# A two-block transformer kernel: order of the first transfers and products, and buffers in two rings

## The chip, the cores and the metric

The kernel runs on one core of a Trainium2 chip. The metric is the device time of one execution in microseconds. Everything is fp32. A core has TensorE for matrix products (in the profile PE, with PEld for the loading of the stationary operand), VectorE (DVE), ScalarE (ACT), GpSimd (POOL), and the queue SyncE (SP), from which this kernel issues all its transfers.

## What is computed

Thirty-two sequences of 64 tokens, width 512, pass through two conditioned blocks. The first is an attention of 8 heads of width 64 that share one head of keys and values, with rotary positions read from an input, and then a gated MLP of width 2048. The second is an attention of 16 heads of width 32 with 4 groups of keys and values that come out of a latent of width 128. Both blocks add their result to their input. The reference, cut to this:

```python
# first block (RMS norm, scaled per sequence by the condition t)
h = rms(x) * (w1 * (1 + t @ tw1.T))
q, k, v = h @ Wq.T, h @ Wk.T, h @ Wv.T      # 8 heads of q, one of k and v
q, k = apply_rope(q, pos_ids), apply_rope(k, pos_ids)
x = x + softmax(q @ k.T / 8) @ v @ Wo.T
h = rms(x) * (w2 * (1 + t @ tw2.T))
x = x + (silu(h @ Wg.T) * (h @ Wu.T)) @ Wd.T
# second block (layer norm, scale and shift from t @ W_ada.T + b_ada)
h = layernorm(x) * (1 + scale) + shift
c = h @ Wkd.T                                # latent of 128
q, k, v = h @ Wq.T, c @ Wku.T, c @ Wvu.T     # 16 heads of q, 4 of k and v
x = x + softmax(rope(q) @ rope(k).T / sqrt(32)) @ v @ Wo.T
```

## The kernel before

**Units.** The 2048 tokens are cut into eight units of 256 tokens (four sequences); activations lie transposed, 128 features by 4 chunks by 256 tokens. `attention0(u)` is the first block's attention of unit u, `mlp(u)` its MLP, `attention1(u)` the second block. Each is a Python generator that records some instructions and yields at places where other work may be put in between. `Order.run` takes pieces of several generators in turn, by planned costs and latencies. The framework beneath then sets the order on each engine itself, following dependencies, its own estimates and the order in which the instructions were recorded; so the order of the trace isn't quite that of the program.

**MLP and its ring of sets.** The MLP uses a scheme of seven block products instead of eight. A set is 128 x 7 x 256 numbers of weight: three parts and four parts worked out from them and a fourth part `a21` (`combine`, L216 to L224, on POOL for the first two sets and otherwise three operations on DVE and one on POOL). In unit 0 a set is loaded as 384 KB (L208) and 128 KB (`a21`, L211, two buffers), combined, and its four worked-out parts are written to DRAM (L229, 512 KB). In the later units they are read back (L213) beside the 384 KB. A unit needs 24 sets, three for each of eight steps q: gate, up, and down of the step before. Sets sit in a ring of `MW = 4` buffers with the tag `mw` (L184); `done_with` asks for the set that goes into a freed buffer. The condition's weights `mod` 0 and 1 sit in the same four buffers before the sets.

**The head.** It runs from the start to the first product of the MLP. SP's transfers come in this order: `small` (condition, vectors, frequencies), `mod` 0, x of unit 0, positions (`pos`, L256), `wqkv` (the weights of queries, keys and values of the first block, 1280 KB in one transfer, L257), x of unit 1, `mod` 1, `wo0`, first sets, `mod` 2 and 3, then the weights of the second block and x of units 2 to 4. `modulation(i)` (L263) makes the scale vectors from the condition. `first_angles` (L339) makes the rotary angles of units 0 and 1 from the positions: about a dozen small operations each on DVE and ACT; `early` (L953) calls it within `attention0(0)`. `angles` (L293) does so for later pairs of units.

In the head both `attention0(0)` and `attention0(1)` are "lean". They square x on ACT (L474), scale x into `h` on DVE and POOL (L482), sum the squares on TensorE (`root_by_quarters`, L447), take the root on ACT (L444) and its reciprocal on DVE (L445), and spread cosine, sine and root over the partitions with small products (`tables_by_quarters`, L387, tiles `tab` and `row`). Only then are the products of queries recorded: first half, keys and values, second half (`project`, L499). Rotations (L507 to L510), transposed values `vt`, scores `sc` (L633), softmax (L519 to L529), transposed probabilities `pp` (L534), context `cx` (L650) and output `po` (L499) follow, then the second norm, whose root (`qs_b`, `row_b`) scales the operands of the MLP, `h` and `hc` (L495, L671 to L674).

The head's order comes from `order.run`: unit 0 has rank 1, unit 1 rank 2, the modulations 1 to 3 rank 3, until unit 0 is done. What is left of unit 1 runs beside `mlp(0)`. From then on `mlp(u)` runs with `attention0(u + 1)` and, one unit behind, `attention1(u - 1)`.

**The ring of x.** A unit's x stays in one of `XB = 5` buffers from its load to its second output store (L550) at the end of `attention1(u)`. `second` then asks for x of unit u + 5.

## Time and profile before

Three runs: median 1082.67 us (1082.35 to 1086.75). The profiled execution took 1086.17 us, of which 1084.1 are its span from the first instruction to the last; the rest lies around the span.

| | busy us | share of the span |
|---|---|---|
| PE (matrix products) | 1026.2 | 95% |
| PEld (weight loads, beside PE) | 948.3 | 87% |
| DVE | 548.7 | 51% |
| ACT | 322.5 | 30% |
| POOL | 434.1 | 40% |
| DMA, mean rate | 183 GB/s | |

The mean granted clock of TensorE is 0.989 of full speed. An engine's busy time is the union of its instructions' spans; matrix products are pipelined and their ends modelled, so a busy PE needn't be at its peak. The chain of waits follows the work back from the last instruction: 69% of it is PE, 11% DVE, 6% DMA, 5% POOL. A wait is put down to what ended last before it.

### The profile page before, as it was taken

The numbers are of one execution on the slowest core, as the hardware profiler recorded it, in microseconds if no ns is written. First come the engines' busy times: TensorE is split into PE (matmuls) and PEld (weight loads), VectorE is DVE, ScalarE is ACT, GpSimd is POOL, SyncE is SP. The second block draws the span as 40 slices with busy tenths as digits, with TensorE's granted clock in tenths as the row PEclk, the third lists the DMA queues.
The fourth block names the chain that finished last, engine by engine and source line by source line (L and its number), as shares of the span: only waits on it lengthen the run. The fifth ranks groups of instructions, "written<-read, shape, count | busy, mean of one in ns | idle before, by whom it ended". The sixth has DMA issues, their size and how long they took to land.

```text
span 1084.1 us, 21449 instructions
## 1 busy us (share of the span) xinstructions
PE 1026.2 (95%) x8538; PEld 948.3 (87%) x8538; DVE 548.7 (51%) x1377; ACT 322.5 (30%) x681; POOL 434.1 (40%) x520
## 2 busy tenths in 40 slices
PE   7899899999999989999999998999999999999887
PEld 6688899998999989999889897999899999998765
DVE  4866466543555475343654368432655344352363
ACT  4421122344124242133422323331424322141132
POOL 4424445443255434254343444324633244331441
PEclk8999999999999999999999999999999999999899
DMA  9717786353655454653646445455635556565001
GB/s 329 262 47 254 265 275 217 140 205 135 210 204 205 159 193 172 234 204 115 223 159 227 174 165 204 156 190 185 234 118 198 175 196 239 188 229 190 11 1 39
DMA packets 68130, 198.53 MB, mean 183 GB/s; under 512 B 7232, under 2 KB 15168, under 8 KB 67520
## 3 DMA queue, kind: packets, MB, share of 16 engines
q1 hardware_dynamic: 68032, 197.17, 52.1%
q8 instruction: 68, 1.11, 0.4%
q14 instruction: 30, 0.25, 0.1%
HBM read 180.37 MB, written 16.78 MB: 182 GB/s over the span
## 4 chain that ended last, share of the span: by engine, by line
PE 69%; DVE 11%; DMA 6%; POOL 5%; issue 2%; ACT 2%; SPq 0%; ACTq 0%; DVEq 0%; POOLq 0%
PE gu L838 27%; PE down L897 14%; PE po L499 10%; PE q L499 8%; DMA set<-in_wmlp 4%; DMA set<-sums 3%; PE pp L534 1%; PE lat L499 1%; PE cx L808 1%; PE sc L784 1%; PE cx L650 1%; DVE mx L519 1%; PE sc L633 1%; DVE sm L527 1%; DVE c L864 1%
## 5 line engine op out<-in xcount | busy, mean ns | idle before, releaser
L838 PE MATMUL gu<-h,set 128*128 128x128 f32 x2048 | 291.3, 278 | 11.8 <-DVE c L857 4.6
L838 PEld LDWEIGHTS gu<-h,set 128*128 128x128 f32 x2048 | 261.4, 193 | 19.3 <-issue 11.9
L838 PE MATMUL gu<-hc,set 128*128 128x128 f32 x1536 | 217.4, 277 | 4.6 <-DVE set L222 2.4
L838 PEld LDWEIGHTS gu<-hc,set 128*128 128x128 f32 x1536 | 194.5, 193 | 6.9 <-DVE set L222 3.6
L876 POOL TENSOR_TENSOR act<-c,c 128x384 f32<-128x384 f32 x64 | 66.5, 1040 | 206.8 <-DVE c L864 148.0
L897 PE MATMUL down<-td,set 128*128 128x128 f32 x1024 | 137.2, 276 | 6.3 <-DMA set<-sums 1.8
L897 PEld LDWEIGHTS down<-td,set 128*128 128x128 f32 x1024 | 125.0, 192 | 9.4 <-issue 3.7
L850 ACT COPY e<-gu 128x128 f32<-128x128 f32 x128 | 33.6, 264 | 303.6 <-PE gu L838 303.1
L499 PE MATMUL po<-cT,wo 128*128 128x256 f32 x480 | 110.8, 384 | 5.8 <-ACT cT L659 3.7
L864 DVE TENSOR_TENSOR c<-gu,u 128x256 f32<-128x256 f32 x128 | 53.4, 419 | 124.0 <-PE gu L838 123.9
L897 PE MATMUL down<-act,set 128*128 128x128 f32 x768 | 110.3, 279 | 3.5 <-DMA set<-in_wmlp 3.2
L852 DVE TENSOR_TENSOR u<-e,gu 128x128 f32<-128x128 f32 x128 | 36.0, 282 | 142.1 <-ACT e L850 141.5
L897 PEld LDWEIGHTS down<-act,set 128*128 128x128 f32 x768 | 97.8, 192 | 9.9 <-DMA set<-in_wmlp 5.8
L499 PEld LDWEIGHTS po<-cT,wo 128*128 128x128 f32 x480 | 90.2, 193 | 18.4 <-ACT cT L659 4.5
L529 POOL TENSOR_TENSOR p<-p,sm 128x512 f32<-128x512 f32 x40 | 40.9, 1042 | 120.2 <-DVE sm L528 114.3
L510 POOL TENSOR_TENSOR qT<-u_q,v_q 128x512 f32<-128x512 f32 x30 | 38.0, 1268 | 95.2 <-DVE v_q L509 95.2
L547 DVE TENSOR_TENSOR x<-x,po 128x512 f32<-128x512 f32 x32 | 22.0, 686 | 76.3 <-PE po L499 76.3
L499 PE MATMUL q<-h,wqkv 128*128 128x256 f32 x256 | 59.1, 382 | 0.8 <-ACT r_a L444 0.8
L933 ACT ACT_TABLE_LOAD x34 | 43.6, 1283 | 44.6 <-DVE c L864 44.3
L499 PEld LDWEIGHTS q<-h,wqkv 128*128 128x128 f32 x256 | 47.2, 190 | 7.4 <-ACT r_a L444 0.9
L499 PE MATMUL q<-h,wq 128*128 128x256 f32 x224 | 52.2, 385 | 1.6 <-POOL h L713 1.6
L878 POOL TENSOR_TENSOR td<-act 128x256 f32<-128x256 f32 x64 | 47.9, 749 | 9.9 <-DVE act L875 3.6
(275 smaller groups left out, 1404.3 us busy)
## 6 DMA issues: line engine op xcount, KB each, us to landing
set<-sums SPq DMA_DIRECT2D x168, 512.0 KB, 5.7
set<-in_wmlp SPq DMA_DIRECT2D x192, 384.0 KB, 4.6
sums<-set SPq DMA_DIRECT2D x24, 512.0 KB, 3.1
x<-in_x SPq DMA_DIRECT2D x8, 512.0 KB, 8.1
out_x<-x SPq DMA_DIRECT2D x16, 256.0 KB, 2.1
mod<-in_mod SPq DMA_DIRECT2D x7, 512.0 KB, 9.9
a<-in_wmlp SPq DMA_DIRECT2D x24, 128.0 KB, 2.9
wo<-in_wo SPq DMA_DIRECT2D x2, 1024.0 KB, 11.0
```

Of the source, the lines that this page charges most:

```text
L499: nc.tensor.matmul(ps, w[:, k, cols], h[:, k, :], start=(k == 0), stop=(k == KC - 1))
L510: nc.gpsimd.tensor_tensor(dst, u, v, ALU.add)
L529: nc.gpsimd.tensor_tensor(p8, p8, sm.unsqueeze(2).to_broadcast(wide), ALU.mult)
L547: nc.vector.tensor_tensor(x[:, part], x[:, part], po, ALU.add)
L838: nc.tensor.matmul(ps, w[:, slot, k * P : (k + 1) * P], b[of][:, k], start=start and k == 0, stop=k == 1, skip_group_check=True)
L850: nc.scalar.copy(e, ps[:, 0])
L852: nc.vector.tensor_tensor(u2, e, ps[:, 1], ALU.add)
L864: nc.vector.tensor_tensor(c.rearrange("p (a b) t -> p a b t", b=2)[:, :, 1], ps[:, 2:4], u2.unsqueeze(1).to_broadcast([P, 2, HT]), ALU.add,)
L876: nc.gpsimd.tensor_tensor(act[:, 1:4], gate[:, 1:4], c[:, 1:4], ALU.mult)
L878: nc.gpsimd.tensor_tensor(td[:, 0:2], act[:, 1:3], act[:, 0:2], ALU.subtract)
L897: nc.tensor.matmul(sums_of[u][p][:, c], w[:, slot, c * P : (c + 1) * P], b[of], start=q % NP == 0 and i % 2 == 0 and c == 0, stop=q % NP = ...
L933: nc.scalar.activation(gate[2][:, 0], gate[0][:, 0], AF.Silu)
```

## The change

- The positions are the first transfer of all. `first_angles` of units 0 and 1 is recorded ahead of `modulation(0)`, and the next pair's positions are asked for behind it.
- `wqkv` becomes two tensors: half of the queries with the keys and values (768 KB), and the other half of the queries (512 KB).
- In the lean units, keys and values and the first half of the queries are projected ahead of the tables; `query` returns its rotation as a function. The first norm's root gets its own small tile `few`. The two halves of the probabilities have a buffer each. The second norm's root and its spreading become two pieces with a yield in between.
- The head isn't planned by `order.run` any more. A string `FIRST` names, piece by piece, which of unit 0 (a), unit 1 (b) and the modulations 1 to 3 (m) is recorded next, and `ordered` ties TensorE's instructions of this stretch to the order of recording, by dependencies without a semaphore.
- The ring of sets has five buffers instead of four, that of x four instead of five.

```diff
+FIRST = "aaaaaaa bb a mm aa b a b aa bbb a b aa a bb a mmmm a bbbb".replace(" ", "")
...
+@contextmanager
+def ordered(tc, engine):
+    traced = tc.nc.cur_bb.bb.instructions
+    start = len(traced)
+    yield
+    mine = [i for i in traced[start:] if i.engine == engine]
+    info = mybir.DependencyInfo(mybir.DependencyClass.NoSync, mybir.DependencyReason.DATA)
+    for one, other in zip(mine, mine[1:]):
+        tc.add_manual_dep(other, one.name, info, reason="order")
...
+    load_positions(0)
     small = fixed("small", [P, C_ALL])
     nc.sync.dma_start(small, a["small"])
...
-    wqkv = fixed("wqkv", [P, KC, 640])
+    wqkv = [fixed("wqkv0", [P, KC, 384]), fixed("wqkv1", [P, KC, 256])]
...
-    XB = 5
+    XB = 4
...
-    MW = 4
+    MW = 5
...
     load_mod(0)
     load_x(0)
...
-    load_positions(0)
-    nc.sync.dma_start(wqkv, a["wqkv"])
+    for i, w in enumerate(wqkv):
+        nc.sync.dma_start(w, a[f"wqkv{i}"])
     load_x(1)
     load_mod(1)
...
+        if tag == "few":
+            return work({"0": "tot0", "1": "kr1"}[room["ring"]], [P, columns], name, 1)
...
         r = yield from norm
-
+        kv, turn = None, None
         if lean:
-            cos, sin, r = tables_by_quarters(u, r, room)
+            few = space(room, "few", 3 * S, f"quarters_{u}").rearrange("p (k c) -> p k c", c=S)
+            root_by_quarters(r, eps0, few[:, 0], f"ms_a{u}")
+            kv = keys_values()
+            yield 1.7, 0.0
+            turn = query(0)
+            yield 3.4, 0.0
+
+        if lean:
+            cos, sin, r = tables_by_quarters(u, few, room)
...
-        query(0)
-        yield 3.4, 0.0
-
-        kv = abank(f"kv0_{u}")
-        project(kv[:, :UT], wqkv, slice(D, D + P), h)
+        turn = turn or query(0)
+        turn(cos, sin)
+        yield 0.0 if lean else 3.4, 0.0
+
+        kv = kv or keys_values()
...
-        by_row(h, root_row(r, eps0, room, f"b{u}") if lean else r)
+        if lean:
+            root = space(room, "r", UT, f"r_b{u}")[:, :S]
+            root_by_quarters(r, eps0, root, f"qs_b{u}")
+            yield 0.3, 2.0
+            r = abank(f"row_b{u}")[:, :UT]
+            spread_out(r.rearrange("p (b s) -> p b s", s=S), root)
+        by_row(h, r)
...
     def early():
-        first_angles(0)
-        first_angles(1)
-        positions.pop()
-        load_positions(2)
         for z in (*vblk0, *vblk1):
             nc.gpsimd.memset(z, 0.0)
...
+    for u in range(2):
+        first_angles(u)
+    positions.pop()
     for _ in modulation(0):
         pass
+    load_positions(2)
...
-    head = [
-        Job(attention0(0, {"ring": "0", "lean": True}, early), A0, 1),
...
-    rest = order.run([*head, others], until=(head[0],))
...
+    ahead = Job(attention0(1, {"ring": "1", "lean": True}, late=lambda: angles(2)), A0)
+    streams = {
+        "a": attention0(0, {"ring": "0", "lean": True, "p": [first[:, :512], first[:, 512:]]}, early),
+        "b": ahead.pieces,
+        "m": other_mods(),
+    }
+    with ordered(tc, mybir.EngineType.PE):
+        for name in FIRST:
+            next(streams[name], None)
+    rest = [ahead]
```

More of the change, by code (lines that the diff above doesn't have):

```diff
@@ L1 @@
-from contextlib import ExitStack
+from contextlib import ExitStack, contextmanager
 import numpy as np
@@ L145, in two_blocks, with load_positions @@
     nc.gpsimd.memset(quarter, float(np.float32(np.pi / 2)))
+    positions = []
+    def load_positions(u0):
+        t = work("pos", [P, 2 * S], f"pos_{u0}", 1).bitcast(I32)
+        nc.sync.dma_start(t, a["pos"][:, u0 * S : (u0 + 2) * S])
+        positions.append(t)
+    load_positions(0)
     small = fixed("small", [P, C_ALL])
@@ L248, in two_blocks @@
     load_x(0)
-    positions = []
-    def load_positions(u0):
-        t = work("pos", [P, 2 * S], f"pos_{u0}", 1).bitcast(I32)
-        nc.sync.dma_start(t, a["pos"][:, u0 * S : (u0 + 2) * S])
-        positions.append(t)
-    load_positions(0)
-    nc.sync.dma_start(wqkv, a["wqkv"])
+    for i, w in enumerate(wqkv):
+        nc.sync.dma_start(w, a[f"wqkv{i}"])
     load_x(1)
@@ L385, in tables, with tables_by_quarters @@
         return cos, sin
-    def tables_by_quarters(u, parts, room):
-        few = work("pT0", [P, 512], f"quarters_{u}", 1).rearrange("p (k c) -> p k c", c=S)
+    def tables_by_quarters(u, few, room):
         r = few[:, 0]
-        root_by_quarters(parts, eps0, r, f"ms_a{u}")
         nc.vector.tensor_tensor(
@@ L557, in attention0, with query, turn, keys_values @@
         h = tile4(room, "h", f"h0_{u}")
+        def query(i):
+            q = abank(f"q0_{u}_{i}").rearrange("p (c t) -> p c t", c=2)
+            for c in range(2):
+                project(q[:, c], wqkv[i], slice(c * P, (c + 1) * P), h)
+            two = [P, 2, UT]
+            def turn(cos, sin):
+                cos, sin = (t.unsqueeze(1).to_broadcast(two) for t in (cos, sin))
+                rotate(qT[:, 2 * i : 2 * i + 2], q, cos, sin, two, f"q0_{u}_{i}")
+            return turn
+        def keys_values():
+            kv = abank(f"kv0_{u}")
+            project(kv[:, :UT], wqkv[0], slice(2 * P, 3 * P), h)
+            return kv
         norm = rms(u, s0a, h, room, f"a{u}")
@@ L570, in attention0 @@
         qT = tile4(room, "qT", f"qT0_{u}")
-        def query(i):
-            q = abank(f"q0_{u}_{i}").rearrange("p (c t) -> p c t", c=2)
-            for c in range(2):
-                project(q[:, c], wqkv, slice((2 * i + c) * P, (2 * i + c + 1) * P), h)
-            two = [P, 2, UT]
-            rotate(
-                qT[:, 2 * i : 2 * i + 2],
-                q,
-                cos.unsqueeze(1).to_broadcast(two),
-                sin.unsqueeze(1).to_broadcast(two),
-                two,
-                f"q0_{u}_{i}",
-            )
-        query(0)
-        yield 3.4, 0.0
-        kv = abank(f"kv0_{u}")
-        project(kv[:, :UT], wqkv, slice(D, D + P), h)
+        turn = turn or query(0)
+        turn(cos, sin)
+        yield 0.0 if lean else 3.4, 0.0
+        kv = kv or keys_values()
         ku = work("u", [P, 512], f"ku_{u}")[:HD0, :UT]
@@ L608, in attention0 @@
         nc.scalar.copy(kb[HD0:], kb[:HD0])
-        yield 1.7, 0.0
-        query(1)
+        yield 0.0 if lean else 1.7, 0.0
+        query(1)(cos, sin)
         yield 3.4, 0.0
@@ L620, in attention0 @@
         yield 0.3, 4.5
-        p = space(room, "p", 1024, f"p0_{u}").rearrange("p (c r k) -> p c r k", r=2, k=S)
+        if lean:
+            ps = [space(room, "p", 512, f"p0_{u}_{t}") for t in range(2)]
+        else:
+            both = space(room, "p", 1024, f"p0_{u}")
+            ps = [both[:, t * 512 : (t + 1) * 512] for t in range(2)]
         for ts in ((0,), (1,)) if lean else ((0, 1),):
@@ L639, in attention0 @@
                         )
-            softmax(banks, HD0**-0.5, f"0_{u}_{ts[0]}", p[:, KC * ts[0] : KC * (ts[-1] + 1)])
+            p = ps[ts[0]] if lean else both
+            softmax(banks, HD0**-0.5, f"0_{u}_{ts[0]}", p.rearrange("p (c r k) -> p c r k", r=2, k=S))
             yield 0.5 * len(ts), 5.0 * ts[0] if lean else 10.0
-        p = p.rearrange("p (t c) r k -> p t (c r k)", t=2)
         cT = tile4(room, "h", f"cT0_{u}")
         for t in range(2):
-            pT = turned(p[:, t], f"0_{u}_{t}", space(room, "pT", 512, f"pT0_{u}_{t}")).rearrange("p (c t) -> p c t", c=KC)
+            pT = turned(ps[t], f"0_{u}_{t}", space(room, "pT", 512, f"pT0_{u}_{t}")).rearrange("p (c t) -> p c t", c=KC)
             yield 0.5, 1.2
@@ L665, in attention0 @@
         r = yield from rms(u, s0b, h, room, f"b{u}")
-        by_row(h, root_row(r, eps0, room, f"b{u}") if lean else r)
+        if lean:
+            root = space(room, "r", UT, f"r_b{u}")[:, :S]
[4 more added lines that the diff above has]
+        by_row(h, r)
         sums = work("hc", [P, 3, 2, HT], f"hc_{u}", 2)
@@ L975, in two_blocks @@
     load_mod(3)
-    head = [
-        Job(attention0(0, {"ring": "0", "lean": True}, early), A0, 1),
-        Job(attention0(1, {"ring": "1", "lean": True, "p": [work("pw", [P, 1024], "p0_1", 1)]}, late=lambda: angles(2)), A0, 2),
-    ]
-    others = Job(other_mods(), 5.4, 3)
-    rest = order.run([*head, others], until=(head[0],))
-    if others in rest:
-        rest.remove(others)
-        order.run([others])
+    first = work("p0", [P, 1024], "p0_0", 1)
+    ahead = Job(attention0(1, {"ring": "1", "lean": True}, late=lambda: angles(2)), A0)
[8 more added lines that the diff above has]
+    rest = [ahead]
     for w, key in ((wq1, "wq1"), (wkd, "wkd"), (wkv1, "wkv1"), (wo1, "wo1")):
@@ L992, in two_blocks @@
     homes["now"] = ("at",)
-    head[1].rank = 0
     def behind():
@@ L1004, in two_blocks @@
         if u == 0:
-            must.append(head[1])
+            must.append(ahead)
         elif u + 1 < NU:
@@ L1108 @@
         "mod": np.ascontiguousarray(lay_mod.reshape(P, KC, 4, D).transpose(2, 0, 1, 3)),
-        "wqkv": _lay(np.concatenate([wq0, wk0, i["L0_cond_Wv"]], 0)),
+        "wqkv0": _lay(np.concatenate([wq0[:256], wk0, i["L0_cond_Wv"]], 0)),
+        "wqkv1": _lay(wq0[256:]),
         "wo0": _lay(i["L0_cond_Wo"]),
```

## The prediction

> **What bounds the kernel now.** I read the busy time by stretch first, then TensorE's waits, the chain of waits, and the timeline of the first 75 us. Busy time by stretch (columns: stretch, length, busy us of PE, weight load, DVE, ACT, POOL, then granted clock, DMA share, GB/s):

> ```profile
> 0.00:9.50 9.50, 6.60 (x54) 5.75 (x54) 0.00 (x0) 1.28 (x1) 3.44 (x20) 1.00 0.78 240
> 9.50:13.10 3.60, 1.57 (x35) 1.02 (x33) 3.11 (x10) 2.13 (x7) 2.16 (x3) 0.56 0.97 399
> 13.10:17.00 3.90, 3.82 (x12) 2.66 (x12) 3.59 (x10) 3.81 (x12) 1.94 (x3) 0.53 1.10 389
> ...
> 31.00:54.00 23.00, 18.72 (x269) 15.18 (x268) 19.02 (x47) 9.77 (x19) 9.47 (x9) 1.00 0.73 264
> 54.00:58.00 4.00, 4.00 (x12) 3.23 (x11) 3.90 (x12) 0.63 (x1) 1.92 (x2) 0.57 0.39 149
> ...
> 71.20:154.00 82.80, 76.07 (x658) 72.83 (x657) 55.99 (x159) 14.53 (x36) 35.05 (x47) 1.00 0.71 236
> 154.00:1009.00 855.00, 831.01 (x6844) 779.57 (x6843) 413.24 (x1033) 258.95 (x534) 342.74 (x400) 1.00 0.54 189
> 1009.00:1084.00 75.00, 60.60 (x463) 48.34 (x461) 36.52 (x77) 21.28 (x51) 27.31 (x26) 0.95 0.04 15
> ```

> TensorE is the engine of the middle (831 of 855 us), so only its idle time and slow clock can be won. They sit in three places: the head before the first MLP product at 71.29 us, MLP unit 0 (71 to 154), and thin gaps later. The tail (1009 on) belongs to units 6 and 7; no edit shortens it.

> **Head.** The timeline of the first units' attention:

> ```profile
> 13.18 3.73 PE L499 MATMUL kv<-h,wqkv 128*128 128x256 f32 x8 [1.22 <-DVE few L352]
> ...
> 15.68 0.31 ACT L444 ACTIVATE quarters<-ms_a,eps 128x64 f32<-128x64 f32 x1
> ...
> 17.66 0.54 DVE L445 RECIPROCAL quarters<-quarters 128x64 f32<-128x64 f32 x1
> ...
> 25.06 0.69 DVE L507 TENSOR_TENSOR v_q<-q,cs 128x512 f32<-128x512 f32 x1 [3.45 <-PE q L499]
> ...
> 37.46 1.16 PE L633 MATMUL sc<-kblk,qT 64*64 64x64 f32 x64
> ...
> 53.64 8.86 PE L499 MATMUL po<-cT,wo 128*128 128x256 f32 x32 [2.66 <-ACT cT L659]
> ```

> Unit 0's sums of squares (ms_a) were ready at 11.96, their root only at 15.99 and its reciprocal at 18.20, because ACT and DVE stood in the angles (9.97 to 20.9). Its scores began at 37.46 although its last qT was done at 32.6: unit 1's products ran in between.

> **MLP unit 0 and after.** The longest pieces of the chain of waits in 71:154 (start, us, what), then two rows of the weight-load queue's waits in 154:1009 (total, times, longest):

> ```profile
> 87.05 4.18 DMA set<-in_wmlp
> 97.71 4.92 DMA set<-in_wmlp
> 108.67 5.63 DMA set<-in_wmlp
> 120.37 6.12 DMA set<-in_wmlp
> ```
> ```profile
> PEld down L897 <- DMA set<-in_wmlp: 5.4, 9, 1.1
> ...
> PEld gu L838 <- DMA set<-sums: 2.7, 3, 1.0
> ```

> Once per period of three sets the chain runs through a set's load: its ring slot comes free too late.

> **The change, part by part.**

> *Positions and angles first.* pos moves from fourth to first in SP's queue, ahead of small and mod. Its 64 KB at the 399 GB/s of 9.5:13.1 cost 0.16 us, its issue 0.43 us (mod0's issues move by that; landing is bandwidth-bound). I take 0.3 us lost at the start of modulation(0). Gained: small landed at 2.9, so with pos the angles' 6.6 us of DVE and some 4.4 us of ACT lie in 3 to 11 us, where the rows show DVE at 0.00 of 9.5. Then sqrt follows ms_a: 12.0 + table load 1.28 + 0.31 + reciprocal 0.55 = 14.2 instead of 18.2. A second sqrt load (30.53, 1.28 us) goes, since no sine stands between the two units' roots. What is late next is TensorE. The angles issue nothing on POOL; pos(2), now behind modulation(0) in the program, still waits only for the casts, and SP has the same transfers ahead of it. If this cover failed (angles running into x's arrival at 9.9), ACT's squares would slip by at most the last sine's 1.3 us table load.

> *wqkv in two.* Landing was 13.05 for 1280 KB. The first 768 KB land 512 KB earlier, 1.3 us at 399 GB/s, so 11.7 to 11.9; but POOL finishes its half of h at 12.42, so kv starts at 12.5, not 13.18: 0.7 gained at most. [...] The row has 399 GB/s with 512 KB transfers one behind another. [...] by the row only one more issue (0.5 us on SP, hidden by a full queue). I take the row: nothing lost.

> *TensorE's order.* Unit prices: a 256-column product 0.216 us (32 po in 6.91 at full clock at 728 us), 128 columns 0.112; the eight kv at half clock 3.73. Path for unit 0: kv 12.5 to 16.0, first q half (16 x 0.216) to 19.4, tab and row 1.9 to 21.3, cs and r copies on ACT about 1.0, rotation from 22.3 (before 25.06). From 21.3 to the first MLP operand TensorE has: second q half 3.46, ms and kv of unit 1 2.4, vt 0.4, modulation(1) 1.4, scores 1.2, unit 1's q 6.9, tab and row 1.9, pp 0.9, cx 1.7, vt 0.4, po 6.9, unit 1's scores 1.2, qs 0.65, modulations 2 and 3 2.8, row_b 0.9: 33.2, so 54.5 without a wait. Waits I can see: scores for qT (DVE 22.3 to 28.8 for seven kv and q operations and two rotations, POOL 1.27, so 30.1 against TensorE's 29.0) 1.1; po for cT 0.7; qs for x and its squares 0.6; two transposes of modulation rows 1.0: 3.4. DVE is the new neighbour: rotations 13, two softmaxes 9.4, set sums 3.8, x, h and modulation rows some 4.7: 31 us in the same 36, so I add 2.5, between nothing and the 8.8 us of angles(2) in between. gu's operands: 60.4 + by_row 1.2; the four last pieces of unit 1 (pp, cx: 2.6) fill TensorE to 63.0. Before, at 71.3, those were done and ten po of unit 1 (2.2) too: 71.3 - 63.0 - 2.2 = 6.1. I take **6**, from 2 (DVE sets the pace) to 9 (no DVE wait).

> kv and q now hold two PSUM banks some 8 us longer, of eight: no wait that I can place, cost 0. The order adds no semaphore, but a piece that waits holds every later piece of both units.

> A fixed order can make an idle TensorE slow. The row: the 2.66 us gap before po, then clock 0.57 in 54:58 and 8.86 instead of 6.91 for it, so a wait of 2.66 cost 4.6. [...] The row decides. My waits are at most 1.1 each[...]; two waits of the row's kind would take 9.2 and with that the head's gain.

> *Five sets.* In a q period TensorE spends 84 x 0.112 = 9.4 us: gate and up first parts to 3.6, half of down to 5.4, their last parts 6.7 and 8.05, rest of down 9.4. With four slots set n frees n+4: up's set is freed at 6.7 and needed at 9.4 + 1.8 (4.5 us later), down's 4.9, gate's 9.4. With five: down's 6.3, gate's 10.8, up's 11.2. A load takes 0.4 to issue, 4.2 to 6.1 to land (the chain's pieces), in unit 0 some 1.7 of sums: 6.3 to 8.2. Down's tightest slack thus still falls up to 1.9 short, less what attention fills. TensorE is idle 6.7 of unit 0's 82.8 us; from start to start against the 0.112 pitch its waits for sets are 4.6 on loads and 3.5 on DVE's sums, 8.1. I take **5.5** of it. Low end 2: at a 9.4 us period the stretch moves 3.15 MB per period (three times 384 and 128 KB in, 512 KB out), 334 GB/s, near the 399 seen. High end 8.1. The prefetch sits in SP's queue before attention's late loads, in 55 to 77 us, when DMA is idle; a21 has still two buffers, so its load waits for the sums two sets back, as before.
> Later (154:1009) a load needs no sums: 0.4 + 5.7 (median set<-sums) fits 6.3. All waits listed are at most 1.1, and the least slack grows by 1.8. 8.1 us of them; I take **4.5**, as TensorE then meets DVE c, POOL td or ACT c (1 to 2 us each in the same list). Ends: -3 (a new order of issue) and 8.

> *Four x.* Reload of slot u+4 now follows unit u's second output store. Stores at 290, 439, 583, 732; reload lands 4 to 7 later; units 4 to 7 first read x at 374, 498, 619, 768: slack 77, 52, 31, 30 us. SP waits for a store's landing once more (2.7 at most), hidden by sets now fetched ahead. Cost 0.

> *The rest* (probabilities in two halves, root and spread as two pieces, `few` in another buffer) issues the same operations: 0.

> **Sum.** 6 + 5.5 + 4.5 = 16 of the profiled execution's 1086.17 (span 1084.1 and 2 around it): 1070. The runs' median is 1082.67, so **1067**.

> **Rivals.**
> A. Only the ring pays (head gains 1): 10 + 1 gives 1072. For it: DVE is 19.02 of 23 busy in 31:54, and moving TensorE's order doesn't move DVE's. Against: 6.6 us of angles leave the crowded part.
> B. Only the head pays: unit 0 becomes bound by DVE (55.99 of 82.8 busy, 9.5 of 10 in 70:80) and by DMA; 6 + 1.5 gives 1075. Against: DVE idled 14.8 us for set loads there.
> C. The fifth set also takes the weight load's unnamed waits on gu and down (7.7 and 6.1 us in 154:1009): 16 + 10 gives 1057.
> D. Slower: four x. Attention of units 6 and 7 must read x whose slot unit 2 or 3 of the second block still holds. If that second block runs late, attention0(6) and (7) start late, and the MLP units behind them. It decides from 30 us of lateness; at three q periods (some 45 us with attention) each is 15 late, 30 in all: 1082.67 - 16 + 30 = 1097. For it: slack shrinks with each unit. Against: second blocks keep their place in the plan, and 30 us is two periods.
> E. The order does nothing on the chip, since before's was as good: same as A.

> **Chances.** Forecast (1062 to 1070) 0.50; A 0.18; B 0.13; C 0.10; D 0.09. A measurement here tells 0.5% (5.4 us) from no change. A falls with faster; of B half does not reach 1077.3. Faster 0.85, within 0.5% 0.07, slower 0.08. Range: all of the forecast, A and most of B and C: 1057 to 1078.

> **What would show it.** sqrt of unit 0 by 14, its scores by 31, po by 45, first gu by 63. In unit 0 the chain's set pieces gone or under 2 us each. In 154:1009 no row of TensorE on set above 1 us in total, PE idle there under 20 of 24. x read at once after landing would show D. I am wrong if first gu stays past 69, if DVE's rows take over TensorE's waits in unit 0, or if attention0(7) waits for x.

## The result, and the profile after

The changed kernel takes 1066.76 us (median of four runs, 1065.94 to 1068.25) against 1082.53 for the kernel before beside it (1082.35 to 1086.75): ratio 0.9847 with the interval 0.9819 to 0.9874, about 16 us less. The sum, 16, was met. Its parts were not: the ring of sets brought far more in the later units than forecast, and the head brought nothing on top of it that can be measured. The profiled execution took 1067.54 us, span 1065.8.

Busy time by stretch, of the kernel after (stretch, length, busy us and count of PE, weight load, DVE, ACT, POOL, then granted clock, DMA share, GB/s):

```profile
0.00:9.50 9.50, 5.46 (x32) 5.01 (x35) 4.54 (x18) 3.84 (x15) 4.49 (x22) 0.97 0.68 212
...
31.00:54.00 23.00, 20.52 (x182) 17.47 (x172) 20.74 (x47) 7.33 (x16) 10.66 (x12) 1.00 0.74 261
...
60.20:70.40 10.20, 8.47 (x57) 6.83 (x58) 6.58 (x21) 3.27 (x7) 3.85 (x4) 0.50 0.00 2
69.92:153.62 83.70, 81.33 (x702) 78.90 (x701) 53.01 (x153) 17.37 (x42) 35.37 (x47) 1.00 0.70 236
153.62:893.40 739.78, 725.37 (x5997) 682.50 (x5996) 371.34 (x918) 232.41 (x473) 304.90 (x351) 1.00 0.55 190
893.40:990.70 97.30, 96.09 (x819) 91.85 (x818) 40.13 (x108) 26.48 (x61) 37.74 (x48) 1.00 0.58 202
```

The same three last stretches of the kernel before, cut at the same instructions: the first gate/up product, the 441st (eight before the end of unit 0's), the end of unit 6 and the end of unit 7.

```profile
71.29:157.74 86.45, 79.58 (x688) 76.20 (x687) 57.91 (x166) 14.79 (x37) 35.77 (x48) 1.00 0.72 241
157.74:906.00 748.26, 729.38 (x5998) 683.95 (x5997) 371.50 (x919) 232.17 (x473) 304.36 (x351) 1.00 0.54 187
906.00:1008.80 102.80, 97.83 (x816) 91.97 (x815) 39.73 (x106) 26.34 (x60) 37.65 (x48) 1.00 0.55 194
```

The reader is to see three things. The angles did move: DVE has 4.54 us of work in the first 9.5 us, where it had none. A long piece at clock 0.50 has appeared at 60 to 70 us. And from 153.62 on TensorE does the same work in less time: in the last of these stretches its idle time fell from 4.97 to 1.21 us.

Unit 0's stretch holds 702 products now and 688 before: 14 of unit 1's products of 256 columns, 3.0 us at 0.216, have moved from the head into it. With them put back, the ledger of the two profiled executions is:

| stretch | before | after | gained | forecast |
|---|---|---|---|---|
| head, to the first gate/up product | 71.29 | 69.92 | 1.4 - 3.0 = -1.6 | 6 |
| unit 0, to its 441st | 86.45 | 83.70 | 2.75 + 3.0 = 5.8 | 5.5 |
| units 1 to 6 | 748.26 | 739.78 | 8.5 | 4.5 for both |
| unit 7 | 102.80 | 97.30 | 5.5 | |
| tail | 75.30 | 75.10 | 0.2 | 0 |
| sum | 1084.1 | 1065.8 | 18.3 | 16 |

**The ring.** The chain of waits on the profile's page of the kernel after:

```profile
PE 78%; DVE 10%; POOL 5%; ACT 2%; DMA 2%; issue 2%; SPq 0%; ACTq 0%; POOLq 0%; DVEq 0%
```

DMA's 6% is 2%, and PE has gone from 69% to 78%. In unit 0 the loads did not leave the chain (kernel after, start, us, what):

```profile
102.39 4.84 DMA set<-in_wmlp
...
114.92 5.29 DMA set<-in_wmlp
...
126.36 2.93 DMA set<-in_wmlp
```

Yet TensorE hardly waits for them: measured from start to start against the usual pitch, its idle time in this stretch fell from 10.4 to 4.7 us. The 4.6 on loads and the 3.5 on DVE's sums fell to 0.3; 2.2 on DVE's c (0.5 before) and 0.8 on ACT's c came instead.

In the later units no wait for a set is left. TensorE's waits for sets in the kernel before, 154 to 1009 us (total, times, longest), and then the whole list of the kernel after, 147 to 990 us, which has none:

```profile
PE down L897 <- DMA set<-in_wmlp: 3.1, 5, 1.0
PE gu L838 <- DMA set<-sums: 2.1, 3, 0.8
PE down L897 <- DMA set<-sums: 1.8, 4, 0.7
```
```profile
PE gu L875 <- DVE c L894: 5.2, 3, 1.8
PE pp L549 <- POOL p L544: 4.0, 3, 2.7
PE gu L875 <- ACT c L970: 3.3, 2, 1.7
PE down L934 <- POOL td L916: 2.2, 4, 1.2
PE q L514 <- ACT r_a L459: 0.8, 1, 0.8
```

**The head.** Timeline of the kernel after:

```profile
14.57 2.93 PE L514 MATMUL kv<-h,wqkv 128*128 128x256 f32 x6 [1.43 <-DVE h L497]
...
15.90 0.31 ACT L459 ACTIVATE quarters<-ms_a,eps 128x64 f32<-128x64 f32 x1
...
32.26 1.16 PE L664 MATMUL sc<-kblk,qT 64*64 64x64 f32 x64
...
47.45 7.17 PE L514 MATMUL po<-cT,wo 128*128 128x256 f32 x32 [0.35 <-ACT cT L690]
```

Keys and values start at 14.57, later than before (13.18), and wait for h; the rotation follows at 24.01. From there the new order does run ahead: scores 5.2 us earlier than before, the output products 6.2. Then the lead is lost, from their end at 54.6 to the first gate/up product at 69.92. Two groups of lines show where. At the start, DVE in the kernel after, and then the same two operations in the kernel before:

```profile
11.25 0.29 DVE L292 COPY rows<-ps_mod 128x128 f32<-128x128 f32 x1 [2.79 <-PE ps_mod L284]
11.45 0.21 DVE L379 TENSOR_TENSOR turns<-few,turns 128x64 f32<-128x64 f32 x1
...
13.56 0.23 DVE L384 TENSOR_TENSOR angle<-few 128x64 f32<-128x64 f32 x1 [1.00 <-ACT few L383]
...
13.84 0.68 DVE L497 TENSOR_TENSOR h<-x,s0a 128x512 f32<-128x512 f32 x1
```
```profile
9.59 0.29 DVE L277 COPY rows<-ps_mod 128x128 f32<-128x128 f32 x1 [9.59 <-PE ps_mod L269]
...
10.83 0.69 DVE L482 TENSOR_TENSOR h<-x,s0a 128x512 f32<-128x512 f32 x1
```

From the copy of modulation rows to h pass 2.59 us; before it was 1.24. The copy stands in the middle of the angles in DVE's queue and waits 2.79 us for modulation(0)'s product. The operation at 11.45 had its operand since 8.46 and still ran only behind the copy. The last steps of both units' angles come behind it, and one of them waits 1.00 us for a sine on ACT, with h queued behind. So the angles were not done by 11 us.

And behind the output products, TensorE in the kernel after:

```profile
57.03 1.06 PE L284 MATMUL ps_mod<-mod,small 128*32 128x128 f32 x32
60.81 0.48 PE L295 MATMUL pt_mod<-ident,rows 128*128 128x128 f32 x1 [2.73 <-DVE rows L292]
61.22 1.94 PE L284 MATMUL ps_mod<-mod,small 128*32 128x128 f32 x32
63.60 0.47 PE L295 MATMUL pt_mod<-ident,rows 128*128 128x128 f32 x1 [0.44 <-DVE rows L292]
63.87 1.81 PE L389 MATMUL row_b<-r_b,spread 128*128 128x64 f32 x8
```

The transposes of modulation rows wait 2.73 us, since DVE stands in unit 1's softmax and unit 0's h and root, and takes the rows only at 60.54. row_b has had its operand, DVE's reciprocal of 60.08 to 60.62, but the given order keeps it behind two modulations until 63.87. The wait also ends in half clock, so that row_b takes 1.81 (1.00 at full clock in after_again).

### The profile page after: what moved, and what is told of

Its sections match the earlier page's. It is cut to its first block, busy times and chain, and to the rows that moved or that the text cites. A ratio compares the mean times of both kernels' runs of the same rounds, so it can differ in the third digit from the quotient of the medians.

```text
span 1065.8 us, 21435 instructions
## 1 busy us (share of the span) xinstructions
PE 1020.6 (96%) x8538; PEld 949.2 (89%) x8538; DVE 548.3 (51%) x1377; ACT 324.9 (30%) x682; POOL 434.9 (41%) x520
## 4 chain that ended last, share of the span: by engine, by line
PE 78%; DVE 10%; POOL 5%; ACT 2%; DMA 2%; issue 2%; SPq 0%; ACTq 0%; POOLq 0%; DVEq 0%
PE gu L875 32%; PE down L934 15%; PE po L514 10%; PE q L514 9%; PE pp L549 2%; PE lat L514 1%; PE cx L845 1%; PE sc L821 1%; PE cx L681 1%; DMA set<-in_wmlp 1%; PE kv L514 1%; PE sc L664 1%; DVE mx L534 1%; DVE sm L542 1%; DMA mod<-in_mod 1%
## 5 line engine op out<-in xcount | busy, mean ns | idle before, releaser
L875 PE MATMUL gu<-h,set 128*128 128x128 f32 x2048 | 289.8, 278 | 10.8 <-DVE c L894 6.8
L514 PE MATMUL po<-cT,wo 128*128 128x256 f32 x480 | 108.4, 380 | 2.4 <-ACT cT L854 2.1
L514 PEld LDWEIGHTS po<-cT,wo 128*128 128x128 f32 x480 | 89.3, 190 | 14.2 <-ACT cT L854 2.6
```

Source lines behind the costliest of these rows:

```text
L514: nc.tensor.matmul(ps, w[:, k, cols], h[:, k, :], start=(k == 0), stop=(k == KC - 1))
L875: nc.tensor.matmul(ps, w[:, slot, k * P : (k + 1) * P], b[of][:, k], start=start and k == 0, stop=k == 1, skip_group_check=True)
```

## The experiments

Each ratio is against the kernel before, run on the same chip; before took 1085.47 us in the first four runs, 1084.19 in the next four and 1085.96 in the last.

**1. ring_only: the kernel before with the two rings changed.** To make room, the lean units' probabilities have two halves, as in the change.

```diff
-    XB = 5
+    XB = 4
...
-    MW = 4
+    MW = 5
...
-        p = space(room, "p", 1024, f"p0_{u}").rearrange("p (c r k) -> p c r k", r=2, k=S)
+        if lean:
+            ps = [space(room, "p", 512, f"p0_{u}_{t}") for t in range(2)]
```

> The kernel before with five sets and four x, and nothing else but the two halves of the probabilities kept in two buffers, which makes the room. Theory R (the ring carries the whole gain, the new head none): 1082.5 - 14 to 17, so 1066 to 1069; no wait of TensorE on a set above 1 us in total, the first MLP product still at about 71 us. Theory P (the prediction's split, 10 of 16 from the ring): 1072 to 1073. Theory H (the head's order carries most): 1076 or more.

Measured: 1063.86 us, 0.9824 (0.9795 to 0.9853). With the old head the rings alone give the whole gain or more, and more than the 14 to 17 us that theory R had named. The halves of the probabilities act in the head alone; they were not tried apart. Three of the four loads in the chain over unit 7's MLP, kernel before:

```profile
939.05 5.43 DMA set<-in_wmlp
...
972.96 6.17 DMA set<-sums
...
990.23 6.63 DMA set<-in_wmlp
```

and the summary by line of the same view of ring_only, shares of its unit 7:

```profile
by line: PE gu L842 48.0%; PE down L901 24.6%; PE po L499 7.1%; PE q L499 7.1%; PE sc L788 2.9%; PE cx L812 2.1%; PE pp L534 1.8%; PE lat L499 1.8%; POOL act L880 1.0%; POOL td L882 0.8%; POOL td L883 0.5%; PE kv L749 0.5%; DVE c L868 0.4%;
```

No set is left in it. Unit 7 takes 102.80 us before and 97.30 in ring_only, the same as in the kernel after. In ring_only no work has moved between the stretches, so its profiled execution gives the ring's share without a correction: 4.7 us in unit 0, 10.3 in units 1 to 6 and 5.5 in unit 7. Its head, with nothing of the new one, came out 1.7 us shorter than before's (in ring_again, below, 1.8 longer).

**2. head_only and four_sets: the change without the fifth set,** with five x and with four.

```diff
-    XB = 4
+    XB = 5
...
-    MW = 5
+    MW = 4
```

> The changed kernel with four sets and five x as before. Theory R: 1081 to 1085, as the head gains nothing or loses up to 2, and the chain in MLP unit 0 runs through the set loads again, 4 to 6 us each. Theory P: 1076 to 1077. Theory H: 1072 or less.

> The changed kernel with four sets and four x. Four x cost nothing by the prediction and by theory R: then this is within 1 us of the run with four sets and five x. If the shorter ring of x costs something by itself, this one is slower than that by 3 us or more, with unit 6 or 7's squares starting as x lands.

Measured: head_only 1082.93 us, 0.9986 (0.9967 to 1.0005), four_sets 1081.89 us, 0.9965 (0.9947 to 0.9983). On four sets the head is worth 1.5 us with five x, which isn't clear of noise (the interval reaches 1.0005), and 4 with four x. Four_sets differs from the change by the fifth set alone, which is thus worth 13 us by the ratios and 15 by the medians. Four x cost nothing: the kernel with fewer x is, if anything, the faster. TensorE's waits in four_sets show the loads back:

```profile
PE down L934 <- DMA set<-sums: 5.2, 11, 0.7
```

A ring of five sets with five x was not tried.

**3. untied: the change with TensorE's order left to the framework.** The order of recording is still that of `FIRST`.

```diff
-    with ordered(tc, mybir.EngineType.PE):
-        for name in FIRST:
-            next(streams[name], None)
+    for name in FIRST:
+        next(streams[name], None)
```

> The changed kernel without the ties between TensorE's instructions, the order of recording kept. If the order of recording does the work: within 1.5 us of the changed kernel's 1066.8. If the ties cost (TensorE held at a piece that waits): 1063 to 1065, with the spreading of the second norm's root ahead of modulation 3. If the ties bring the gain: 1072 or more.

Measured: 1062.95 us, 0.9803 (0.9774 to 0.9833), 4 us less than the change by the medians and 5 by the ratios. The intervals of the ratios overlap a little (the change's begins at 0.9819), but every run of untied (1061.02 to 1063.74) is below the change's first four, and of after_again's six one alone (1062.26) is not above them. So tying the order, with the string the same, costs. In the trace few places differ. A part of unit 1's scores goes before po, and both modulations are taken together, with one wait of 1.86 us behind them in place of the 2.73. Earlier, unit 0's transposed probabilities (pp) wait for POOL; the given order keeps unit 1's tables behind them although their operands are ready, and untied takes most of the tables first. TensorE in the kernel after, then in untied:

```profile
38.66 0.66 PE L549 MATMUL pp<-ident,p 128*128 128x128 f32 x4 [1.58 <-POOL p L544]
39.15 1.06 PE L389 MATMUL tab<-quarters,spread 128*128 128x128 f32 x8
```
```profile
36.00 1.05 PE L389 MATMUL tab<-quarters,spread 128*128 128x128 f32 x8
...
37.72 0.66 PE L549 MATMUL pp<-ident,p 128*128 128x128 f32 x4 [0.28 <-POOL p L544]
```

That is 1.3 us of the 4, and from keys and values to po untied takes 31.60 us against 32.88. Behind po the first gain, row_b 6.35 us after po's end instead of 9.24, is not all kept: in untied half clock runs from 59.6 to 66.4, and the first gate/up product comes at 64.18. Where the rest of the 4 us arises isn't shown.

**4. after_again, mod2_early, scores_early: the same kernel once more, and two other orders,** of which mod2_early takes modulation 2 ahead of the last pieces, and scores_early spreads the modulations and takes a piece of unit 1 forward.

```diff
-... aa bbb a b aa a bb a mmmm a bbbb
+... aa bbb a b mm aa a bb a a mm bbbb          (mod2_early)
+... aa bbb m a m b m a bb m aa a bb a bb      (scores_early)
```

> The changed kernel once more, beside the next three. Between profiled executions the head's length varies (weights of modulation 0 landed at 7.9 to 9.3 us, half-clock stretches fall differently), so the first MLP product may stand at 64 to 70 us. Ratio to the kernel before 0.980 to 0.987; if the ties cost as much as one comparison suggests, it stays 3 to 5 us above the untied kernel's 0.9803.

> The changed kernel with modulation 2's two pieces ahead of unit 0's output and modulation 3's behind row_b: FIRST ends in 'a b mm aa a bb a a mm bbbb'. Theory G (the head gives its gain back behind the output: the operands wait in h2 for modulation 2's weights, and TensorE stands before the modulations' transposes and goes to half clock): 3 to 6 us faster than the changed kernel run beside it, row_b about 7 us after the end of po instead of 9.2. Rival (VectorE sets this stretch anyway): within 1 us.

> The changed kernel with modulations 2 and 3 spread ahead of and within unit 0's output, unit 1's scores between its halves and one context of unit 1 ahead of row_b: FIRST ends in 'm a b m a bb m aa a bb a bb', with the pieces before as before. Theory G: 4 to 8 us faster than the changed kernel, as unit 1's softmax on VectorE then lies under the output's 7 us of TensorE. Rival: within 1 us, or slower if the second half of the output is held by the scores' wait for unit 1's queries.

Measured: after_again 1066.76 us, 0.9851 (0.9828 to 0.9874); mod2_early 1066.92, 0.9845 (0.9822 to 0.9868); scores_early 1065.24, 0.9833 (0.9809 to 0.9858). Neither order helps. In mod2_early row_b follows the end of the output products after 5.1 us instead of 9.2, but it waits 2.5 us for DVE's reciprocal there, and the first gate/up product comes at 70.69: unit 1's transposes and context run before it at half clock, from 59.2 to 72.9. The wait was moved, and its clock with it. In scores_early the squares of unit 0's second norm are waited for instead, 2.2 us, and half clock runs from 60.9 to 71.2.

after_again is worth most as a second profiled execution of the same kernel: first gate/up product at 64.61 instead of 69.92, time 1062.26 instead of 1067.54. By po after_again leads by 1.7 us (45.77 against 47.45), by row_b by 2.8 (61.08 against 63.87), at the first gate/up product by 5.3; from po's end on, these 3.6 us are the clock, below. At the 441st gate/up product 3.4 us are left (150.26 against 153.62), and at the end it is 5.3 again; after has a stretch of half clock at 254.7 that after_again hasn't.

**5. angles_late: angles back in their place behind the keys and values of unit 0;** the positions stay the first transfer.

```diff
     def early():
+        first_angles(0)
+        first_angles(1)
+        positions.pop()
+        load_positions(2)
...
-    for u in range(2):
-        first_angles(u)
-    positions.pop()
```

> The changed kernel with the positions still first in SP's queue, but the angles of units 0 and 1 recorded where they were, behind the squares of unit 0. If the angles in front cost the start (VectorE's half of h stood behind a sine's product until 13.84 us): keys and values start 1 us or more earlier relative to modulation 0's landing, and the time falls by 1 to 2 us. If they pay as predicted (root 4 us earlier): 2 to 3 us slower than the changed kernel.

Measured: 1062.01 us (1058.48 to 1067.67), 0.9809 (0.978 to 0.9837). DVE in angles_late:

```profile
10.69 0.29 DVE L292 COPY rows<-ps_mod 128x128 f32<-128x128 f32 x1 [3.75 <-PE ps_mod L284]
...
11.95 0.68 DVE L497 TENSOR_TENSOR h<-x,s0a 128x512 f32<-128x512 f32 x1
```

1.26 us from the copy to h instead of 2.59, keys and values at 12.69, unit 0's root at 14.12 instead of 15.90. Modulation 0's weights land at different times in each execution (see the end), so the fair measure is from their landing: keys and values start 3.5 us behind it, against 5.3 in after and 5.6 in after_again. The root that the change was to bring forward comes earlier without the moved angles than with them.

**6. ring_again, late_untied, norm_first, norm_first_untied: what is the head worth on top of the ring?** ring_again is the kernel of ring_only. late_untied has the edits of angles_late and untied together. norm_first is angles_late with unit 0's norm ahead of unit 1's scores and softmax:

```diff
-... aa bbb a b aa a bb a mmmm a bbbb
+... aa bbb m a b m aa a a mm a bb
```

> The kernel before with the ring of five, four x and the probabilities in halves (as ring_only). Theory R (nearly all of the change's gain is the ring's; on top of it the new head is worth nothing that can be measured): 0.982 +- 0.002 of before, 1064 us, first gate/up product at 69 to 70, the stretch behind the first 440 of these products 910 us. Rival (the new head is worth the 1.5 to 4 us more that head_only and four_sets showed): 0.984 to 0.986 and above the two kernels late_untied and norm_first beside it by 3 us or more.

> after with the angles and positions of unit 1 back behind the keys and values of unit 0 (as in angles_late) and TensorE's order of the first two units' pieces left to the program. Theory G (two costs of the head of after stand beside each other: the angles ahead of modulation 0 on VectorE, 2 to 4 us, and the given order, 2 to 4 us): both gone, 1058 to 1061 us, ratio 0.976 to 0.979. Rival (they are one and the same few us, or lie within what the start varies by): as angles_late and untied, 0.980 to 0.982. Keys' and values' first product near 12.7, first gate/up product 62 to 64 in both.

> angles_late with the given order changed: modulation 2's pieces are spread ahead of unit 0's po, unit 0's norm pieces stand before unit 1's scores and softmax, and the last four pieces of unit 1's attention are left to run beside unit 0's MLP. Theory N (behind po the norm chain of unit 0 stands behind unit 1's softmax on VectorE, two table loads on ScalarE, and modulation 2's operands): first gate/up product at 59 to 60 instead of 64, and 3 to 5 us less than angles_late, 1057 to 1059, ratio 0.976 to 0.978. Rival (unit 1's work is only moved into unit 0's MLP, where VectorE and the score banks hold it): first product early, but the end of unit 0's 440 products as in angles_late (147.8 +- 1), ratio 0.981 +- 0.001.

> norm_first with TensorE's order left to the program (the order of issue alone is changed). Theory N: the few places in which the given order differs cost nothing here, as norm_first, 1057 to 1059, ratio 0.976 to 0.978. Theory G (the given order costs 2 to 4 us wherever it stands): 2 to 4 us below norm_first. Rival of N: as late_untied, within 1 us.

| | us (range) | ratio (interval) | first gate/up | its 441st |
|---|---|---|---|---|
| ring_again | 1065.36 (1062.13 to 1070.22) | 0.9817 (0.9783 to 0.9851) | 73.12 | 154.73 |
| late_untied | 1058.49 (1056.94 to 1059.88) | 0.9750 (0.9721 to 0.9779) | 61.19 | 146.17 |
| norm_first | 1063.85 (1061.77 to 1065.09) | 0.9796 (0.9766 to 0.9826) | 58.12 | 149.05 |
| norm_first_untied | 1063.99 (1061.52 to 1066.25) | 0.9803 (0.9769 to 0.9837) | 59.12 | 151.10 |

late_untied is the fastest kernel of the study, 27 us under before, where the change has 16; its slowest run is faster than ring_again's fastest. The two costs that angles_late and untied took away one at a time do add: 4 to 5 us each, 8.3 together. For ring_again theory R had the ratio right (0.982), but late_untied beats it by 6.9 us, and R had the head worth nothing. Row_b follows po's end sooner in late_untied than in angles_late, 6.29 us against 8.07 (TensorE, late_untied):

```profile
55.58 0.33 PE L295 MATMUL pt_mod<-ident,rows 128*128 128x128 f32 x1 [1.86 <-DVE rows L292]
55.74 1.00 PE L389 MATMUL row_b<-r_b,spread 128*128 128x64 f32 x8
...
60.69 0.66 PE L549 MATMUL pp<-ident,p 128*128 128x128 f32 x4 [1.59 <-POOL p L544]
```

But the last line takes this back: unit 1's transposed probabilities wait 1.59 us for POOL, and the first gate/up product comes 11.74 us after po's end, against 11.59 in angles_late, both at full clock. The lead of late_untied in these two traces lies ahead of po: from keys and values to po 30.31 us against 32.53, of which 1.3 are the wait of pp named under untied and 0.8 less half clock at the start.

Theory N fell, and its rival came nearer. norm_first does bring the first gate/up product to 58.12, 5.9 us before that of angles_late (63.98), but the end of the 440 products is 1.3 us later (149.05 against 147.80). The stretch between holds 12 of unit 1's products more and more waits. TensorE's longest waits there in norm_first (total, times, longest):

```profile
PE gu L875 <- DVE c L894: 1.6, 4, 0.5
PE pp L549 <- POOL p L544: 1.5, 1, 1.5
PE gu L875 <- DVE hc L710: 1.0, 1, 1.0
```

All that is listed sums to 6.3 us, against 2.5 in angles_late. DVE has 64.40 us of work in that stretch instead of 55.24, and the head's lead is repaid. Theory G, that the given order costs 2 to 4 us wherever it stands, found no support: norm_first with and without it take the same time. Yet pp waits 1.58 us with it and 0.30 without it here too, and norm_first_untied's runs had a lower mean clock (0.9875 against 0.991), which can hide a gain. In norm_first the wait of the transposes ahead of row_b is 0.44 us; that the order costs most where a long wait stands there was argued, not tried by itself.

## Why the prediction was right in sum and wrong in its parts

Its own signs say as much. In the kernel after, none of the four times named for the head was met: root by 14 (15.90), scores by 31 (32.26), po by 45 (47.45), first gate/up product by 63 (69.92). "I am wrong if first gu stays past 69" came true in this execution, though not in after_again's (64.61). The signs of the later units were all met: no wait for a set is listed, TensorE is idle 15.6 us (under 20), and x is not read as it lands.

- **Unit 0's ring, 5.5: right**, 5.8 by the ledger and 4.7 in ring_only. The step that I feared, DVE's rows in the place of the loads', took 2.2 us for c, as against 8.1 that went. The sign that I had named, set pieces under 2 us in the chain, was a bad one: they still stand there at 2.93 to 5.29 us. A chain can run through a load and the combining behind it without TensorE being idle for it.
- **Later units, 4.5 with an upper end of 8: wrong, 14.0.** Two terms were mis-sized. The listed waits gave 8.1, but from start to start TensorE's gaps on set loads over units 1 to 7 were 10.0 us in before, and none are left; gaps with no named releaser fell by some 2.5 besides. And I struck off almost half because TensorE would "meet DVE c, POOL td or ACT c" next. It did not: from before to after these went from 5.0 to 5.7, from 3.7 to 2.9, and stayed at 3.6. 5.5 of the 14 us lie in unit 7 alone (0.9 to 2.9 in each of the others, from before to ring_only); its MLP has no next unit's attention beside it that could fill the wait for a set, which fits but was not tried. I had spread the gain evenly. Rival C had the size (10 us more behind the head), but its cause, the unnamed waits, made up only some 2.5 of it.
- **The head, 6 with ends at 2 and 9: wrong, -1.6 in the profiled execution, and 3.7 in after_again's** (71.29 - 64.61 - 3.0). Beside the predicted path (keys and values 12.5, po 45, first gate/up product 63.0) the kernel after lost 2.1 us by keys and values, 0.4 more by po and 4.5 behind it; after_again lost 0.5, 0.3 and 0.8. Four products more than forecast also moved out of the head. Three steps failed. "0.3 us lost at the start of modulation(0)": in DVE's queue the angles cost h 1.35 us (2.59 against 1.24), as "the angles' 6.6 us of DVE in 3 to 11" forgot that they alternate with ACT and stand around a copy that waits. "14.2" for the reciprocal of unit 0's root: 16.80, as the root itself stood behind the sine's table load (1.28 us from 11.97) and sines on ACT until 15.90. And of my waits of "at most 1.1 each" the one for modulation rows, put at 1.0 for two transposes, took 2.73 and 0.44. The warning that stood beside them, that a piece that waits "holds every later piece of both units", was left at no price; dropping the ties gave 4 to 5 us.
- **Half clock.** I had read the row of before, a gap of 2.66 us that cost 4.6, and taken it as the price of such a wait; but I had charged nothing, since no wait of mine was that long. One came that was, 2.73, and in this execution the row was right in kind: half clock from 60.2 to 70.4, which cost 3.6 us on top of the wait (from po's end to the first gate/up product 15.29 us against 11.66 in after_again). In angles_late's and after_again's the same wait of 2.73 left the clock alone; how the windows of after and after_again differ is told below.
- **Four x** cost nothing, as forecast (four_sets against head_only); in the kernel after x of units 4 to 7 landed 77, 52, 30 and 29 us before its first read, where 77, 52, 31 and 30 had been forecast, so rival D is out; **wqkv in two** was not tried by itself; in no trace of the new head did keys and values wait for their weights, and in ring_again, with one transfer, they did for 0.9 us.

So rival A's mechanism, only the ring pays, is what the change as it stands does; its time, 1072, was built on the small ring. That the forecast of 1067 met 1066.8 was luck: two errors of opposite sign, 9.5 us too little for the later units and 7.6 too much for the head.

The parts do not add: 0.9824 for the rings and 0.9965 for the head would give 0.979, or 23 us, and the change has 16. The head was not without worth: late_untied lies 6.9 us under ring_again, near the 6 that I had put on it (its mean clock was higher too, 0.9915 against 0.9875). Which of its remaining edits, positions first, wqkv in two, keys ahead of the tables or the order of recording, brings this was not tried apart. Angles_late gains more (4 to 5 us, with intervals that overlap) than the 1.9 to 2.1 us that its keys and values start earlier behind the weights' landing. The clock takes part in it. Within a kernel the runs' times go with their mean granted clock: angles_late from 1058.5 us at 0.992 to 1067.7 at 0.982, the change's ten runs from 1062.3 at 0.992 to 1068.8 at 0.982. Angles_late's mean is 0.988 and the change's 0.9855; at 0.6 to 0.9 us per 0.001, as within these two kernels, an estimated 2 us of the gain go with it. Untied had the change's clock (0.985), so its 4 us are not of this kind. Why one kernel falls into half clock more often than another was not tried.

## What to carry to other kernels

Price a ring by the slack between a slot's release and its next need, and take waits from start to start, unit by unit: where a unit lacks filler work, as unit 7 here (5.5 us), the whole shortfall can show. An operation moved to an idle stretch of an engine must be finished before the first waiting instruction of that engine's queue, its partner engine's work included; otherwise what waits takes the moved work along (here DVE's angles, 1.35 us on h). Before giving an engine a fixed order, look for the piece with the longest wait and ask what ready work stands behind it.

## What the runs showed of the hardware

```profile
56.80:60.20 3.40, 1.28 (x63) 1.01 (x52) 3.37 (x8) 3.35 (x4) 1.23 (x2) 1.00 0.34 123
60.20:63.60 3.40, 2.35 (x34) 1.58 (x34) 1.80 (x6) 1.16 (x3) 0.85 (x1) 0.50 0.01 2
```
```profile
54.80:58.20 3.40, 1.53 (x64) 1.26 (x64) 3.36 (x8) 3.10 (x5) 1.23 (x2) 1.00 0.45 169
58.20:61.60 3.40, 2.02 (x40) 1.64 (x40) 2.46 (x8) 2.12 (x3) 1.53 (x2) 1.00 0.01 2
```

In the first, the window holds 2.1 us of idle time and the next is at half clock; in the second the same wait is cut by the grid, with 1.9 and 1.4 us idle in two windows, and the clock stays. Over fourteen traces, up to 1040 us, a window at full clock with more than 1.9 us of idle time of TensorE was followed by half clock every time (33 windows, the longest idle for 2.66 us), one with 1.3 to 1.9 sometimes, one with less than 1.25 never. Before and after have seven of the first kind (2.10 to 2.66 us); of their twelve with 1.4 to 1.8, those with 1.49, 1.50 and 1.75 were followed by half clock, and nine were not. At half clock, a window with 0.6 us or more idle was followed by another every time (33 windows), one with less than 0.1 by full clock every time (51); between these both happened (in after, 0.15 and 0.49 by another, 0.19 by full clock), so idle time alone doesn't decide it. What sets the clock was not shown beyond these counts. With the same 2.73 us wait, one execution of this kernel paid 3.6 us behind po that another did not, and the place of the grid is the difference that their windows show. A wait of this size in a head can thus be worth more than its length.

**The first modulation's weights land at different times.** The second half of `mod` 0 landed at 8.43 us in before, 9.24 in after, 7.46 in after_again and 9.22 in angles_late, and over the fourteen traces between 7.24 and 9.25, whichever order the transfers had. Differences of 1 to 2 us at the start of a single trace say nothing of an edit.
